# A sparse graph attention layer on one core: tiles of more than 16 slots in two chunks, the weighted sum in slot 0's buffer, the scatter behind the next gathers

## Chip, cores and metric

The kernel runs on one core of a Trainium2 chip. The metric is the device time from the first to the last instruction, in microseconds (us), as the median of several runs; less is better. The engines are TensorE (PE in the profile), VectorE (DVE), ScalarE (ACT), GpSimd (POOL) and SyncE (SP). POOL here does little arithmetic in the part that matters: it issues the indirect transfers (gathers and scatters of rows), one after the other and in a fixed order.

## What is computed

The reference is one layer of graph attention over 3327 nodes with 1024 features each:

```python
h = jnp.maximum(_layernorm(x, axis=-1), 0.0)
f = h @ Wf + bf
g = h @ Wg + bg
e = jax.nn.relu(f @ g.T)
scores = jnp.where(adj > 0, e, NEG)            # NEG = -9e15
attention = jax.nn.softmax(scores, axis=1)
x = x + attention @ (h @ W + bW)
```

The adjacency matrix is sparse: a node has some 16 neighbours, at most a few dozen. So the kernel doesn't compute 3327 x 3327 scores. It makes a list of neighbours for every node and gathers their rows.

## The kernel before

The first part, up to about 300 us, reads `x` and `adj`, writes the normalised rows to memory (`hd`), finds each node's neighbours, and sorts the nodes by their number of neighbours. It also multiplies the two score weights into one matrix, so that a score is a dot product of a projected row q with the plain row of a neighbour. There is a dense version of the whole layer too, which runs only where a node has more neighbours than the lists hold; it doesn't run on these inputs.

The second part works on 26 tiles of 128 nodes each, from many neighbours to few. `CAPS` has the number of slots of each tile: how many neighbours the node with the most of them has.

```python
CAPS = [37, 25, 23, 22, 21, 21, 20, 20, 19, 19, 18, 18, 17, 17, 17, 16, 16, 15, 15, 15, 14, 14, 13, 13, 12, 11]
ONE_CHUNK = 20
AHEAD = 3
```

For each slot k of a tile, one indirect transfer gathers 128 rows (512 KB) into a buffer G, and VectorE makes the 128 dot products with q:

```python
gpool = ctx.enter_context(tc.tile_pool(name="G", bufs=23))
ypool = ctx.enter_context(tc.tile_pool(name="y", bufs=2))
xpool = ctx.enter_context(tc.tile_pool(name="xp", bufs=2))

def prepare(s):                       # cut: the PSUM groups and the mask
    gather(pi, pd[:, :], perm[:, s : s + 1])        # neighbour lists
    gather(hp, hd[:, :], perm[:, s : s + 1])        # own rows
    ...                                             # TensorE: transpose hp, q = hp @ A   (line 667)

def dot(s, k):
    e = st[s]
    g = G[s, k] = gpool.tile([P, D], FP, name="G")
    gather(g, hd[:, :], e["pi"][:, k : k + 1])
    junk = jpool.tile([P, D], BF, name="junk")
    nc.vector.tensor_tensor_reduce(                 # line 684
        junk, g, e["q"][:, :D], 1.0, e["q"][:, D : D + 1], op0=ALU.mult, op1=ALU.add,
        accum_out=e["sc"][:, k : k + 1],
    )
```

After the last dot of a chunk the scores go through a softmax. A tile in two chunks keeps the maximum and the sum of the first, and rescales the weighted sum y when the second has a greater maximum:

```python
def softmax(s, k0, k1, last):         # cut: to what a second chunk adds
    ...
    if k0:
        nc.vector.tensor_tensor(nm, nm, e["nm"], op=ALU.min)
    nc.scalar.activation(sc, sc, AF.Exp, bias=nm, accum_out=l)
    if k0:
        nc.scalar.activation(al, e["nm"], AF.Exp, bias=nm, scale=-1.0)
        nc.vector.scalar_tensor_tensor(l, e["l"], al, l, op0=ALU.mult, op1=ALU.add)
    ...
    if k0:
        nc.scalar.activation(e["y"], e["y"], AF.Copy, scale=al)      # line 711
```

Then the rows are added up with their weights. Slot 0 is scaled into y by ScalarE, most others are added by VectorE, and some slots of the tile's last chunk are scaled by ScalarE and added by TensorE, which transposes at the same time:

```python
def on_tensor(s, k0, k1):
    m = min(max(0, CAPS[s] - 13), k1 - k0 - 2)
    ks = range(max(k0, 1), k1)
    return [k for i, k in enumerate(ks) if (i + 1) * m // len(ks) > i * m // len(ks)]

def combine(s, k0, k1, last):
    e = st[s]
    if not k0:
        e["y"] = ypool.tile([P, D], FP, name="y")
    y = e["y"]
    e["first"] = True
    pe = on_tensor(s, k0, k1) if last else []
    for k in range(k0, k1):
        p = e["sc"][:, k : k + 1]
        g = G[s, k]
        if k in pe:
            nc.scalar.activation(g, g, AF.Copy, scale=p)             # line 741
            sum_transposed(e, g, e["first"], False)                  # TensorE, line 725
            e["first"] = False
        elif k == 0:
            nc.scalar.activation(y, g, AF.Copy, scale=p)             # line 745
        else:
            nc.vector.scalar_tensor_tensor(y, g, p, y, op0=ALU.mult, op1=ALU.add)   # line 747
```

TensorE transposes y on top of its own sum and multiplies with W; the result gets the rows of x by an accumulating gather and is scattered to the output:

```python
def project(s):                       # cut
    sum_transposed(e, e["y"], e["first"], True)
    ...                                                              # yT @ W, line 759
    r = e["r"] = xpool.tile([P, O], FP, name="res")
    ...
            nc.scalar.copy(r[:, o * CB : (o + 1) * CB], ps)          # line 761

def finish(s):
    e = st[s]
    gather(e["r"], x[:, :], perm[:, s : s + 1], compute_op=ALU.add)
    ins = nc.gpsimd.indirect_dma_start(out=out[:, :], ..., in_=e["r"], ...)   # line 767
```

The order in which the work is written down:

```python
for s, cap in enumerate(CAPS):
    half = (cap + 1) // 2
    units += [(s, 0, half), (s, half, cap)] if cap > ONE_CHUNK else [(s, 0, cap)]

prepare(0)
prepare(1)
for i, (s, k0, k1) in enumerate(units):
    last = k1 == CAPS[s]
    dots(s, range(k0, k1))
    if not k0 and s:
        finish(s - 1)
    softmax(s, k0, k1, last)
    if i + 1 < len(units):
        s2, a, b = units[i + 1]
        dots(s2, range(a, min(b, a + AHEAD)))
    combine(s, k0, k1, last)
    if last:
        project(s)
        if s + 2 < NT:
            prepare(s + 2)
```

The framework puts each engine's instructions in a final order at build time: among those that its own model of time holds ready, the one written first goes first. It also hands out the buffers of a pool from those that are free at that point, not in turn. On the chip each engine then works strictly in that order.

Of the kernel before, what the change touches and what calls it, by code (L numbers as in the profile page):

```python
# [8 lines left out]
FP = mybir.dt.float32  # L9
I32 = mybir.dt.int32  # L10
AF = mybir.ActivationFunctionType
ALU = mybir.AluOpType
# [10 lines left out]
NBIN = 64  # L23

CAPS = [37, 25, 23, 22, 21, 21, 20, 20, 19, 19, 18, 18, 17, 17, 17, 16, 16, 15, 15, 15, 14, 14, 13, 13, 12, 11]
ONE_CHUNK = 20
AHEAD = 3
LAG = 4

# [260 lines left out]
def edge_path(ctx: ExitStack, tc: tile.TileContext, x, adj, Wf, bf, Wg, bg, W, bW, out, flag):  # L290
# [10 lines left out]
    nc = tc.nc  # L301
    N, D = x.shape
    O = W.shape[1]
    P = 128
# [21 lines left out]
    hd = dram.tile([N, D], FP, name="hd")  # L326
# [15 lines left out]
    perm = const.tile([P, NT], I32, name="perm")  # L342
    final = const.tile([P, 1], I32, name="final")
# [7 lines left out]
    with ExitStack() as part1:  # L351
# [73 lines left out]
        def degrees(t):  # L425
            n = rows(t)
            r = kpool.tile([P, N], FP, name="r")
            a = r.bitcast(I32)
            for b, m in pieces(t):
                nc.sync.dma_start(a[b : b + m], adj[t * P + b : t * P + b + m, :])  # L430

            cuts = [0, SEG // 2 * SW, N] if t >= NT - 2 else [0, N]
            for i, (b, e) in enumerate(zip(cuts, cuts[1:])):
                to = deg[:n, t : t + 1] if not i else half[:n]
                nc.scalar.activation(r[:n, b:e], a[:n, b:e], AF.Relu, accum_out=to)  # L435
                nc.gpsimd.tensor_mul(r[:n, b:e], r[:n, b:e], iotaj[:n, b:e])  # L436
                if i:
                    nc.scalar.activation(deg[:n, t : t + 1], deg[:n, t : t + 1], AF.Identity, bias=half[:n])
            return r
# [115 lines left out]
        for t in range(NT):  # L555
            r = degrees(t)
# [63 lines left out]
    W_sb = ctx.enter_context(tc.tile_pool(name="W", bufs=1)).tile([P, KD, O], FP, name="W_sb")  # L620
    nc.sync.dma_start(W_sb, W.rearrange("(k p) o -> p k o", p=P))
    psp = ctx.enter_context(tc.tile_pool(name="ps", bufs=3))
    gpool = ctx.enter_context(tc.tile_pool(name="G", bufs=23))
    hpool = ctx.enter_context(tc.tile_pool(name="hp", bufs=2))
    qpool = ctx.enter_context(tc.tile_pool(name="q", bufs=2))
    hTpool = ctx.enter_context(tc.tile_pool(name="hT", bufs=1))
    ypool = ctx.enter_context(tc.tile_pool(name="y", bufs=2))
    yTpool = ctx.enter_context(tc.tile_pool(name="yT", bufs=1))
    xpool = ctx.enter_context(tc.tile_pool(name="xp", bufs=2))
    jpool = ctx.enter_context(tc.tile_pool(name="junk", bufs=1))  # L630
# [4 lines left out]
    p_o = ctx.enter_context(tc.tile_pool(name="p_o", bufs=2, space=PSUM))  # L635

    def gather(to, table, idx, **kw):
        nc.gpsimd.indirect_dma_start(  # L638
            out=to,
            out_offset=None,  # L640
            in_=table,
            in_offset=bass.IndirectOffsetOnAxis(ap=idx, axis=0),
            **kw,
        )
# [8 lines left out]
    st = {}  # L653
# [23 lines left out]
    G = {}  # L677

    def dot(s, k):
        e = st[s]  # L680
        g = G[s, k] = gpool.tile([P, D], FP, name="G")
        gather(g, hd[:, :], e["pi"][:, k : k + 1])
        junk = jpool.tile([P, D], BF, name="junk")
        nc.vector.tensor_tensor_reduce(  # L684
            junk, g, e["q"][:, :D], 1.0, e["q"][:, D : D + 1], op0=ALU.mult, op1=ALU.add,
            accum_out=e["sc"][:, k : k + 1],
        )

    def softmax(s, k0, k1, last):

        e = st[s]
        sc = e["sc"][:, k0:k1]
        nc.vector.scalar_tensor_tensor(sc, sc, 0.0, e["mask"][:, k0:k1], op0=ALU.max, op1=ALU.add)
        nm = small.tile([P, 1], FP, name="nm")
        nc.vector.tensor_reduce(nm, sc, AX.X, ALU.max, negate=True)
        if k0:
            nc.vector.tensor_tensor(nm, nm, e["nm"], op=ALU.min)
        l = small.tile([P, 1], FP, name="l")
        nc.scalar.activation(sc, sc, AF.Exp, bias=nm, accum_out=l)
        if k0:  # L700
            al = small.tile([P, 1], FP, name="al")
# [3 lines that stand above are left out]
            rs = small.tile([P, 1], FP, name="rs")  # L705
            nc.vector.reciprocal(rs, l)
            if k0:
                nc.vector.tensor_tensor(al, al, rs, op=ALU.mult)
            nc.vector.tensor_scalar(sc, sc, rs, None, op0=ALU.mult)
        if k0:  # L710
            nc.scalar.activation(e["y"], e["y"], AF.Copy, scale=al)
        e["nm"], e["l"] = nm, l
# [7 lines that stand above are left out]
    def sum_transposed(e, g, first, last):  # L720

        if first:
            e["yT"] = p_y.tile([P, KD, P], FP, name="yT_ps")
        for c in range(KD):
            nc.tensor.matmul(  # L725
                e["yT"][:, c, :], g[:, c * P : (c + 1) * P], ident, is_transpose=True,
                start=(first and c % 4 == 0), stop=(last and c % 4 == 3), skip_group_check=True,
            )

    def combine(s, k0, k1, last):  # L730
        e = st[s]
        if not k0:
            e["y"] = ypool.tile([P, D], FP, name="y")
        y = e["y"]
        e["first"] = True
        pe = on_tensor(s, k0, k1) if last else []
# [4 lines that stand above are left out]
                nc.scalar.activation(g, g, AF.Copy, scale=p)  # L741
                sum_transposed(e, g, e["first"], False)
                e["first"] = False
            elif k == 0:
                nc.scalar.activation(y, g, AF.Copy, scale=p)  # L745
            else:
                nc.vector.scalar_tensor_tensor(y, g, p, y, op0=ALU.mult, op1=ALU.add)  # L747

    def project(s):
        e = st[s]  # L750
        yT = yTpool.tile([P, KD, P], FP, name="yT")
        sum_transposed(e, e["y"], e["first"], True)
        for g in range(0, KD, 4):
            nc.scalar.copy(yT[:, g : g + 4, :], e["yT"][:, g : g + 4, :])  # L754
        r = e["r"] = xpool.tile([P, O], FP, name="res")
        for o in range(OH):
            ps = p_o.tile([P, CB], FP, name="ps_o")
            for k in range(KD):
                nc.tensor.matmul(ps, yT[:, k, :], W_sb[:, k, o * CB : (o + 1) * CB], start=(k == 0), stop=False)  # L759
            nc.tensor.matmul(ps, ones3, bW3[:, o * CB : (o + 1) * CB], start=False, stop=True)  # L760
            nc.scalar.copy(r[:, o * CB : (o + 1) * CB], ps)  # L761

    def finish(s):
        e = st[s]

        gather(e["r"], x[:, :], perm[:, s : s + 1], compute_op=ALU.add)
        ins = nc.gpsimd.indirect_dma_start(  # L767
            out=out[:, :],
            out_offset=bass.IndirectOffsetOnAxis(ap=perm[:, s : s + 1] if s < N // P else final, axis=0),
            in_=e["r"],  # L770
            in_offset=None,
            bounds_check=None if s < N // P else N - 1,
            oob_is_err=s < N // P,
        )
        tc.declare_no_dep(ins.ins, group="results", reason="other rows")
        tc.add_to_no_dep_group("results", ins.ins)

# [12 lines left out]
# [3 lines that stand above are left out]
    done = set()  # L793

    def dots(s, ks):
        for k in ks:
            if (s, k) not in done:
                done.add((s, k))
                dot(s, k)
# [3 lines left out]
    for i, (s, k0, k1) in enumerate(units):  # L803
        last = k1 == CAPS[s]
        dots(s, range(k0, k1))
        if not k0 and s:
            finish(s - 1)
        softmax(s, k0, k1, last)
        if i + 1 < len(units):
            s2, a, b = units[i + 1]  # L810
            dots(s2, range(a, min(b, a + AHEAD)))
        combine(s, k0, k1, last)
        if last:
            project(s)
            if s + 2 < NT:
                prepare(s + 2)
            if s + 2 == NT - 1:
                bad = failed()
    finish(NT - 1)
    return bad  # L820


def kernel(tc: tile.TileContext, x, adj, Wf, bf, Wg, bg, W, bW, out):

    nc = tc.nc
    with tc.tile_pool(name="flag", bufs=1) as fpool:
        flag = fpool.tile([1, 1], I32, name="flag")
        bad = edge_path(tc, x, adj, Wf, bf, Wg, bg, W, bW, out, flag)  # L830
        with tc.If(bad > 0):
            dense_path(tc, x, adj, Wf, bf, Wg, bg, W, bW, out)
# [27 lines left out]
```

## Time and profile before

| | |
|---|---|
| time, median of 3 runs | 1418.14 us (1415.55 to 1426.23) |
| span of the profiled run | 1415.5 us |
| VectorE busy | 1221.1 us (86%) |
| TensorE busy | 1172.8 us (83%) |
| POOL busy | 876.6 us (62%) |
| ScalarE busy | 474.8 us (34%) |
| moved by the DMA engines | 372.52 MB, mean 263 GB/s |

A row of the profile's costliest groups gives the source line, the engine and operation, what it writes and reads, the shape and the count; then the busy time of the group, the mean time of one in ns, and how long the engine had stood idle just before them and what ended most of that. A list of waits gives who waited, for whom, the total in us, how often, and the longest. A shape such as `128x1024` is partitions by elements. The time between two scatters to the output (line 767) is a good measure of one tile. Some of them, each with the start of its scatter:

| tile | slots | chunks | scatter at us | since the one before, us |
|---|---|---|---|---|
| 2 | 23 | 2 | 531.98 | 44.4 |
| 3 | 22 | 2 | 575.52 | 43.5 |
| 4 | 21 | 2 | 616.37 | 40.9 |
| 5 | 21 | 2 | 661.43 | 45.1 |
| 6, 7 | 20 | 1 | 707.48, 754.75 | 46.1, 47.3 |
| 8, 9 | 19 | 1 | 803.58, 853.47 | 48.8, 49.9 |
| 10, 11 | 18 | 1 | 898.42, 943.45 | 45.0, 45.0 |
| 12, 13, 14 | 17 | 1 | 982.32, 1022.18, 1059.45 | 38.9, 39.9, 37.3 |
| 15, 16 | 16 | 1 | 1094.20, 1128.78 | 34.8, 34.6 |

### The profile page before, as it was taken

How to read it: one execution, taken by the hardware profiler on the slowest of the kernel's cores; microseconds unless marked ns; L12 is line 12 of the kernel's file. 1: busy time of each engine (PE TensorE's matmuls, PEld its weight loads, DVE VectorE, ACT ScalarE, POOL GpSimd, SP SyncE). 2: the span in 40 equal slices, each digit the busy share in tenths (PEclk: the TensorE clock that was granted, in tenths of full speed). 3: DMA queues.
4: the chain of work that ended last, by engine and by line, in shares of the span. 5: the costliest groups of instructions: out<-in, count | busy, mean ns of one | idle time of the engine just before them, and what ended most of it. 6: DMA issues, size and time to landing. Idle time of an engine off the chain costs nothing.

```text
span 1415.5 us, 14137 instructions
## 1 busy us (share of the span) xinstructions
PE 1172.8 (83%) x4355; PEld 684.0 (48%) x4355; DVE 1221.1 (86%) x2550; ACT 474.8 (34%) x738; POOL 876.6 (62%) x628
## 2 busy tenths in 40 slices
PE   4569998167288999999878977899999999999784
PEld 3544554044165556665545544555555555555331
DVE  4888889919979999998898788889999999999970
ACT  6666776311063244433312321222222222222110
POOL 8677777364666766775556556666667766666501
PEclk9999999578599999999989988999999999999897
DMA  9898796196678999886778667878889888888712
GB/s 370 330 356 307 294 346 229 49 361 236 227 269 289 316 315 330 282 291 224 266 284 277 192 248 265 275 233 266 256 285 304 273 265 255 256 285 286 242 31 61
DMA packets 97710, 372.52 MB, mean 263 GB/s; under 512 B 14268, under 2 KB 14684, under 8 KB 94297
## 3 DMA queue, kind: packets, MB, share of 16 engines
q0 software_dynamic: 79552, 286.85, 60.6%
q1 hardware_dynamic: 10860, 70.49, 13.2%
q10 hardware_dynamic: 7212, 14.18, 2.8%
q8 instruction: 36, 0.59, 0.2%
q14 instruction: 50, 0.41, 0.1%
HBM read 343.67 MB, written 27.80 MB: 262 GB/s over the span
## 4 chain that ended last, share of the span: by engine, by line
issue 26%; DVE 23%; PE 20%; POOL 18%; DMA 9%; ACT 4%; POOLq 0%; ACTq 0%; SPq 0%; DVEq 0%
DVE y L747 11%; POOL r L436 10%; PE ps_o L759 10%; POOL G L638 6%; DVE junk L684 6%; DMA G<-hd,pi 5%; PE ps_q L667 4%; PE yT_ps L725 3%; DMA pi<-pd,perm 2%; ACT G L741 2%; DVE cand L446 2%; PE ps_A L519 1%; DVE sc L684 1%; POOL res L638 1%; ACT r L435 1%
## 5 line engine op out<-in xcount | busy, mean ns | idle before, releaser
L638 POOL DMA_INDIRECT G<-hd,pi x468 | 542.8, 1160 | 260.0 <-issue 99.2
L684 DVE CUSTOM_DVE_ANT_0 junk<-G,q 128x1024 bf16<-128x1024 f32 x468 | 601.1, 1284 | 68.2 <-DMA G<-hd,pi 48.7
L667 PE MATMUL ps_q<-A_sb,hT 128*128 128x342 f32 x1248 | 394.2, 464 | 53.6 <-ACT q L669 43.2
L747 DVE SCALAR_TENSOR_TENSOR y<-G,sc,y 128x1024 f32<-128x1024 f32 x320 | 411.7, 1286 | 8.0 <-ACT y L745 6.1
L759 PE MATMUL ps_o<-W_sb,yT 128*128 128x512 f32 x832 | 387.6, 621 | 9.5 <-ACT yT L754 9.1
L667 PEld LDWEIGHTS ps_q<-A_sb,hT 128*128 128x128 f32 x1248 | 231.4, 193 | 172.3 <-ACT q L669 44.6
L759 PEld LDWEIGHTS ps_o<-W_sb,yT 128*128 128x128 f32 x832 | 161.2, 198 | 208.9 <-issue 190.6
L436 POOL TENSOR_TENSOR r<-r,iotaj 128x3327 f32<-128x3327 f32 (+4 forms) x28 | 188.6, 6740 | 67.0 <-ACT r L435 50.4
L446 DVE MAX8 cand<-r 128x8 f32<-128x208 f32 (+2 forms) x416 | 134.9, 363 | 35.2 <-POOL r L436 35.2
L741 ACT ACTIVATE G<-G,sc 128x1024 f32<-128x1024 f32 x122 | 129.8, 1137 | 0.0
L519 PE MATMUL ps_A<-WgT,WfT 128*128 128x512 f32 x256 | 120.7, 633 | 1.1 <-ACT WfT L490 1.0
L761 ACT COPY res<-ps_o 128x512 f32<-128x512 f32 x52 | 30.4, 585 | 269.2 <-PE ps_o L760 269.2
L725 PE MATMUL yT_ps<-ident,G 128*128 128x128 f32 x976 | 116.5, 275 | 3.2 <-ACT G L741 3.2
L725 PEld LDWEIGHTS yT_ps<-ident,G 128*128 128x128 f32 x976 | 107.0, 140 | 15.8 <-ACT G L741 7.9
L669 ACT COPY q<-ps_q 128x342 f32<-128x342 f32 x78 | 33.5, 450 | 199.3 <-DVE sc L684 94.4
L638 POOL DMA_INDIRECT res<-in_x_dram,perm x26 | 47.0, 1806 | 68.5 <-ACT res L761 65.4
L754 ACT COPY yT<-yT_ps 128x512 f32<-128x512 f32 x52 | 27.8, 587 | 166.4 <-PE yT_ps L725 166.4
L519 PEld LDWEIGHTS ps_A<-WgT,WfT 128*128 128x128 f32 x256 | 51.3, 203 | 65.0 <-issue 62.7
L725 PE MATMUL yT_ps<-ident,y 128*128 128x128 f32 x208 | 35.0, 323 | 52.3 <-DVE y L747 38.8
L435 ACT ACTIVATE r<-r 128x3327 f32<-128x3327 int32 (+4 forms) x28 | 77.5, 2766 | 0.1
L767 POOL DMA_INDIRECT out_dram<-res,perm x25 | 30.2, 1207 | 70.9 <-DMA res<-in_x_dram,perm 70.9
L651 ACT COPY hT<-ps_t 128x512 f32<-128x512 f32 x52 | 29.8, 592 | 117.6 <-PE ps_q L667 72.0
(139 smaller groups left out, 786.7 us busy)
## 6 DMA issues: line engine op xcount, KB each, us to landing
r<-in_adj_dram SPq DMA_DIRECT2D x25, 1663.5 KB, 9.6
xt<-in_x_dram SPq DMA_DIRECT2D x25, 512.0 KB, 10.2
hd<-xt ACTq DMA_DIRECT2D x25, 512.0 KB, 6.6
G<-hd,pi POOLq DMA_INDIRECT x468, 6.1
wr<-in_L_gnn_Wg_dram SPq DMA_DIRECT2D x8, 512.0 KB, 13.7
wr<-in_L_gnn_Wf_dram SPq DMA_DIRECT2D x8, 512.0 KB, 8.9
W_sb<-in_L_gnn_W_dram SPq DMA_DIRECT2D x1, 4096.0 KB, 16.6
r<-in_adj_dram SPq DMA_DIRECT2D x1, 1455.6 KB, 8.8
```

The costliest lines, as they stand in the source:

```text
L435: nc.scalar.activation(r[:n, b:e], a[:n, b:e], AF.Relu, accum_out=to)
L436: nc.gpsimd.tensor_mul(r[:n, b:e], r[:n, b:e], iotaj[:n, b:e])
L446: nc.vector.max(cand[:n, s * 8 : s * 8 + 8], r[:n, s * SW : min(N, (s + 1) * SW)])
L519: nc.tensor.matmul(ps, WfT[:, k, :], WgT[:, k, o * CB : (o + 1) * CB], start=(k == 0), stop=(k == KD - 1))
L638: nc.gpsimd.indirect_dma_start(out=to, out_offset=None, in_=table, in_offset=bass.IndirectOffsetOnAxis(ap=idx, axis=0), **kw,)
L667: nc.tensor.matmul(ps[:, :QB], hT[:, k, :], A_sb[:, k, o : o + QB], start=(k == 0), stop=False)
L669: nc.scalar.copy(q[:, o : o + QB], ps[:, :QB])
L684: nc.vector.tensor_tensor_reduce(junk, g, e["q"][:, :D], 1.0, e["q"][:, D : D + 1], op0=ALU.mult, op1=ALU.add, accum_out=e["sc"][:, k : k ...
L725: nc.tensor.matmul(e["yT"][:, c, :], g[:, c * P : (c + 1) * P], ident, is_transpose=True, start=(first and c % 4 == 0), stop=(last and c % ...
L741: nc.scalar.activation(g, g, AF.Copy, scale=p)
L747: nc.vector.scalar_tensor_tensor(y, g, p, y, op0=ALU.mult, op1=ALU.add)
L759: nc.tensor.matmul(ps, yT[:, k, :], W_sb[:, k, o * CB : (o + 1) * CB], start=(k == 0), stop=False)
```

## The change

Three things change. Tiles of 17 to 20 slots, too, are worked on in two chunks, so that the buffers of a first chunk are free again before all of the tile's dots are done. The weighted sum y isn't kept in a buffer of its own: it is kept in the buffer of slot 0, whose row it starts from, and the memory of the two y buffers goes to G, which gets 25. And the tile's end is issued elsewhere: the accumulating gather of x is written right after the product with W, and the scatter is placed behind the gathers of the next tile's first slots, so that POOL need not stand while the gather lands.

```diff
-ONE_CHUNK = 20
+ONE_CHUNK = 16
...
-    gpool = ctx.enter_context(tc.tile_pool(name="G", bufs=23))
+    gpool = ctx.enter_context(tc.tile_pool(name="G", bufs=25))
...
-    ypool = ctx.enter_context(tc.tile_pool(name="y", bufs=2))
...
     def dot(s, k):
         e = st[s]
         g = G[s, k] = gpool.tile([P, D], FP, name="G")
-        gather(g, hd[:, :], e["pi"][:, k : k + 1])
+        st["gathered"] = gather(g, hd[:, :], e["pi"][:, k : k + 1])
...
     def combine(s, k0, k1, last):
         if not k0:
-            e["y"] = ypool.tile([P, D], FP, name="y")
+            e["y"] = G[s, 0]
...
             elif k == 0:
-                nc.scalar.activation(y, g, AF.Copy, scale=p)
+                nc.scalar.activation(y, y, AF.Copy, scale=p)
...
     def project(s):
...
+        gather(r, x[:, :], perm[:, s : s + 1], compute_op=ALU.add)
+
     def finish(s):
-        e = st[s]
-
-        gather(e["r"], x[:, :], perm[:, s : s + 1], compute_op=ALU.add)
-        ins = nc.gpsimd.indirect_dma_start(
...
+        with tc.issue_after(st["gathered"].ins):
+            ins = nc.gpsimd.indirect_dma_start(
...
     for i, (s, k0, k1) in enumerate(units):
         last = k1 == CAPS[s]
         dots(s, range(k0, k1))
-        if not k0 and s:
-            finish(s - 1)
         softmax(s, k0, k1, last)
         if i + 1 < len(units):
             s2, a, b = units[i + 1]
             dots(s2, range(a, min(b, a + AHEAD)))
+        if last and s:
+            finish(s - 1)
         combine(s, k0, k1, last)
```

`tc.issue_after` orders the issue alone: the scatter goes into POOL's queue behind the last gather written so far, and waits for nothing else than before.

More of the change, by code (lines that the diff above doesn't have):

```diff
@@ L637, in gather @@
     def gather(to, table, idx, **kw):
-        nc.gpsimd.indirect_dma_start(
+        return nc.gpsimd.indirect_dma_start(
             out=to,
@@ L761, in project @@
             nc.scalar.copy(r[:, o * CB : (o + 1) * CB], ps)
+        gather(r, x[:, :], perm[:, s : s + 1], compute_op=ALU.add)
     def finish(s):
-        e = st[s]
-        gather(e["r"], x[:, :], perm[:, s : s + 1], compute_op=ALU.add)
[L767 to L774, printed above, removed]
+        with tc.issue_after(st["gathered"].ins):
+            ins = nc.gpsimd.indirect_dma_start(
+                out=out[:, :],
+                out_offset=bass.IndirectOffsetOnAxis(ap=perm[:, s : s + 1] if s < N // P else final, axis=0),
+                in_=st[s]["r"],
+                in_offset=None,
+                bounds_check=None if s < N // P else N - 1,
+                oob_is_err=s < N // P,
+            )
         tc.declare_no_dep(ins.ins, group="results", reason="other rows")
```

## The prediction

> **What bounds the kernel now.** I read the page's busy times first, then its forty slices, then cut the part that the change touches into stretches and asked for the waits in each.
>
> The page says VectorE (DVE) is busiest with 1221.1 of 1415.5 us, TensorE (PE) second with 1172.8. These are averages over two parts with different work; only the second, from the first gather at 296 us, is touched. From the costliest groups:
>
> ```profile
> L684 DVE CUSTOM_DVE_ANT_0 junk<-G,q 128x1024 bf16<-128x1024 f32 x468 | 601.1, 1284 | 68.2 <-DMA G<-hd,pi 48.7
> L747 DVE SCALAR_TENSOR_TENSOR y<-G,sc,y 128x1024 f32<-128x1024 f32 x320 | 411.7, 1286 | 8.0 <-ACT y L745 6.1
> ```
>
> These are the kernel's two big VectorE operations, one dot product per gathered slot and one weighted add per slot not given to TensorE. The reader is to see that 68.2 us of VectorE idleness stands before the dots, most of it ended by a gather landing. To see where, I cut the second part at scatters of whole tiles, at 616 us (tile 4) and at 1060 us (tile 14). Between these two lie the last two-chunk tile (21 slots) and the nine tiles of 20 to 17 slots, one chunk each today. The columns are start and end, length, then busy time of PE, PEld, DVE, ACT, POOL, then granted clock, DMA share and GB/s:
>
> ```profile
> 487.00:616.00 129.00, 122.63 (x519) 74.97 (x518) 127.32 (x205) 49.91 (x74) 90.13 (x78) 0.99 0.89 307
> 616.00:1060.00 444.00, 396.41 (x1495) 231.85 (x1494) 392.19 (x579) 123.53 (x186) 267.16 (x228) 0.94 0.77 257
> 1060.00:1334.00 274.00, 262.19 (x884) 142.42 (x882) 266.85 (x393) 58.77 (x107) 186.83 (x150) 1.00 0.85 274
> ```
>
> The first row holds three two-chunk tiles (23 to 21 slots): VectorE is 98.7% busy. The last row holds the small one-chunk tiles: 97.4%. The middle row is 88.3%: 51.8 us of VectorE are lost there, at a lower granted clock and with the DMA engines emptier. So the middle is not bound by any engine but by a wait. The waits of that stretch (total us, times, longest):
>
> ```profile
> DVE junk L684 <- DMA G<-hd,pi: 39.3, 25, 3.5
> ...
> POOL G L638 <- ACT y L745: 60.1, 10, 10.6
> ...
> POOL out_dram L767 <- DMA res<-in_x_dram,perm: 31.0, 11, 4.2
> ...
> POOL res L638 <- ACT res L761: 6.7, 6, 1.9
> ```
>
> VectorE waits for gathers, and the gathers' queue (POOL) waits about 6 us per tile for ACT line 745. That line scales slot 0 into y, and it is the first reader to finish with any G buffer of the tile. It cannot run before all dots of the tile and its softmax are done. The event in the queue's timeline, for a tile of 19 slots:
>
> ```profile
> 733.50 1.01 POOL L638 DMA_INDIRECT hp<-hd,perm  x1 [0.31 <-issue]
> 744.52 1.86 POOL L638 DMA_INDIRECT G<-hd,pi  x1 [10.01 <-ACT y L745]
> ```
>
> With this tile's slots and the next tile's first ones, all 23 buffers are full. POOL stands 10 us, and after the first buffer is freed the next gather still needs its landing time (6.1 us median on the page). VectorE meanwhile runs out of gathered rows. In 487 to 616 the same wait does not appear: chunks of 11 to 13 slots give buffers back halfway through the tile.
>
> **What the Trainium skill says.** "Perfetto Trace Analysis", section Optimization Strategy: a gap that recurs on the engine that should be saturated can mean too few buffers for the next tile. The trace agrees: about 5 us of VectorE per tile over ten tiles, with POOL waiting for a buffer. "TensorE: Matmul & The Clock Gate", section What's actually happening: an idle window of about 3.4 us drops the array to half its clock. The trace fits: in the middle stretch PE waits for y up to 6.6 us and the granted clock is 0.94 (0.89 to 0.90 between 707 and 898 us); in the saturated stretches it is 0.99 to 1.00. "DMA: Bandwidth & Descriptors", section Specifications: about 358 GB/s of HBM per core. The two-chunk stretch moves 307 GB/s with DMA engines 89% busy, so there is room, but not much. The same page, section Two DMAs through the same engine are not ordered: a dependent DMA needs its issuer to wait for the first one's semaphore. That is POOL's wait for res at line 767, 75.7 us in the whole trace.
>
> **The change, part by part.**
>
> 1. *Two chunks for 17 to 20 slots.* Nine tiles: 20, 20, 19, 19, 18, 18, 17, 17, 17. Large operations do not change in number. TensorE takes min(CAPS-13, second chunk-2) slots; the second chunks are 10, 10, 9, 9, 9, 9, 8, 8, 8, so CAPS-13 (7 down to 4) still fits. VectorE keeps CAPS dots plus 12 adds.
>  Added per tile on VectorE, from today's two-chunk tiles: a second masked max (0.17 and 0.16 us), a minimum (0.15), the sum's rescale (0.22) and one product (0.16): 0.86 us, nine times 7.7 us. On ACT: two exponentials and one rescale of y (1.15 us), about 1.9 us; ACT is 28% busy there.
>  Removed: the wait for slot 0 until 17 to 20 dots are over.
>  I size this in two ways. (a) By busy share: 392.2 + 7.7 = 399.9 us of VectorE work at the 98.7% of the two-chunk stretch is 405.2 us instead of 444: 38.8 us less. (b) By the rate of large operations. Between 487 and 616 us there are 65.5 dots (two records each) and 37 adds, 102.5 in 129 us: 1.259 us each with all overhead of two chunks. Between 1060 and 1334 there are 217 in 274: 1.263. In the middle there are 192 + 120 = 312 in 444: 1.423. At 1.26 they take 393 us: 51 us less. (a) keeps the busy time that isolated operations show (1.28 us and a record of 0.08), (b) lets dots and adds pair at 2.4 us as they do when VectorE is fed.
> 2. *y in slot 0's buffer, 25 instead of 23 + 2.* The memory is the same. y holds a G buffer until TensorE has transposed it, so 24 or 23 stay for rows. The pool gives out whichever buffer is free, so one that is held does not block those behind it in turn. For tiles up to 16 slots I count 0, at most a few us either way.
> 3. *Scatter behind gathers, accumulate-gather after project.* POOL's wait for res to land (about 2.4 us per tile) goes, and gathers fill it. But POOL is 60 to 70% busy and VectorE 97 to 99% in the stretches without the buffer wait, so it is worth little: 0 to 3 us in all. The accumulate-gather now stands before the rest of the next tile's gathers in program order; its wait for ACT res was only 6.7 us in the middle stretch and may grow.
> 4. *The end.* After 1334 us the last tiles finish on PE and POOL alone. Last res at 1397.2, last scatter at 1403.6, end at 1415.5: this chain has no other work to hide behind and nothing in the change shortens it. 0, with some us of luck in how the last tiles interleave.
>
> Sum: minus 39 to minus 51 from part 1, 0 to minus 3 from the scatter, perhaps 2 to 5 given back by the changeover from two chunks to one, which moves to 17|16. (Today's changeover tile, 616 to 661 us, took 45.1 us where its equal before took 40.9.) I take 43 us off 1418.1: 1375 us.
>
> **The rivals.**
>
> *TensorE becomes the bound.* For: a saturated tile of 21 slots took 40.9 us between scatters (575.5 to 616.4), of which PE was busy 39.0 at clock 1.00. A 20-slot tile has one transposed slot less, near 1.1 us. PE then needs some 38 to 40 us, VectorE 32 operations at 1.26, 40.3 us. They are nearly tied, and in two-chunk tiles all of TensorE's slots fall in the second chunk, so PE gets its work in bursts. Against: the three tiles between 487 and 616 us ran at 1.26 per operation with the same burst. If PE binds at 42 us or the burst costs 1.5 us per tile, 14 us of the gain are lost: 1390.
>
> *The gathers stay the limit.* For: DMA is at 89% when VectorE is fed, and POOL's queue is in order, so a wait for ACT res ahead of the gathers stalls them all. Against: POOL busy 90 of 129 us in the fed stretch, and waits for ACT res of 2 to 3 us did not starve VectorE there. If it bites, 10 to 25 us are lost: 1385 to 1400.
>
> *Chunks cost more than they bring.* The tiles of 17 lose only about 3 us each today (scatter to scatter 38.9, 39.9, 37.3), so a second softmax with its chain through ACT (VectorE to ACT and back, then y's rescale) could make these three no faster. Already half counted; 1380.
>
> **Range and chances.** Sizing (a) with a small loss gives about 1385, (b) with the scatter's help about 1365; both rivals biting together give 1400. Range 1358 to 1400. The 2% line lies at 1389.8, 15 us above my number, a little over one spread of about 14: faster 0.80, same 0.17, slower 0.03. The last would need the issue order of POOL to turn bad in many tiles, for which the profile shows nothing.
>
> **What would show it.** Right: POOL's wait for ACT line 745 falls from 67 to under 15 us; VectorE's wait for gathers falls from 48.7 to under 20; the nine tiles take 37 to 42 us between scatters; granted clock 0.97 or more from 700 to 900; POOL's wait at line 767 is near 15 us (the end only). Wrong: a new large wait of POOL for ACT res, or of PE or VectorE for each other in these tiles; or tiles of 16 and fewer slots slower than their 34 to 36 us because y holds a buffer; or a longer end.

## Result, and the profile after

The changed kernel takes 1369.88 us (median of four runs, 1367.98 to 1371.97) against 1416.85 us for the kernel before beside it (1414.42 to 1426.23). The ratio is 0.9657, with a 95% interval of 0.961 to 0.9704. A later repeat on another chip gave 0.9658.

The first rows to look at are again VectorE's two large operations, from the costliest groups of the changed kernel. The two numbers after the bar are busy time and mean time of one, then comes the idle time before them:

```profile
L683 DVE CUSTOM_DVE_ANT_0 junk<-G,q 128x1024 bf16<-128x1024 f32 x468 | 599.4, 1281 | 35.3 <-ACT q L668 18.1
L746 DVE SCALAR_TENSOR_TENSOR G<-G,sc 128x1024 f32<-128x1024 f32 x320 | 410.8, 1284 | 4.6 <-ACT G L744 4.1
```

Counts and durations are what they were. What went is idle time: before the dots it is 35.3 us instead of 68.2, and gathers no longer head the list of what ended it. Over the whole span VectorE's idle time is 1370.1 - 1218.5 = 151.6 us; before it was 1415.5 - 1221.1 = 194.4. That is 42.8 of the 45.4 us by which the two profiled spans differ.

To see where, the span is cut at the scatters of the same tiles as before: 0, 4, 14 and 22.

| stretch between scatters | before, us | after, us | difference |
|---|---|---|---|
| start to tile 0 (37 slots, two chunks in both) | 439.33 | 445.96 | +6.6 |
| tiles 1 to 4 (two chunks in both) | 177.0 | 176.7 | -0.4 |
| tiles 5 to 14 (nine of the ten changed to two chunks) | 443.1 | 386.7 | -56.4 |
| tiles 15 to 22 (16 to 13 slots, one chunk in both) | 274.1 | 276.7 | +2.6 |
| tile 22 to the end | 82.0 | 84.1 | +2.1 |

The sum is -45.4 us. The whole gain lies where the change was aimed, though not all of the 56.4 is gain. At a cut VectorE is already ahead with the next tiles' dots, and with two chunks it is less far ahead. By the counts of the groups it does 189 dots and 116 adds in the third stretch, 305 in place of 312; 221 instead of 217 in the fourth, and 34 instead of 31 in the last. Seven large operations, some 9 us, are passed on. What remains is about 47 us of gain in the third stretch, and the last two are no slower than their extra operations explain. Whether the first row is the change's isn't shown: the changed kernel, profiled again, has that scatter at 446.7 us, and four programs that differ from it only in later tiles have it at 437 to 442 us.

The same cut with busy times (columns as in the prediction: start and end, length, busy time of PE, PEld, DVE, ACT, POOL, granted clock, DMA share, GB/s), for the changed kernel:

```profile
494.00:623.00 129.00, 122.69 (x518) 74.98 (x517) 127.32 (x203) 49.91 (x74) 90.63 (x80) 0.99 0.90 312
623.00:1009.00 386.00, 375.36 (x1493) 222.35 (x1492) 380.90 (x616) 138.74 (x222) 264.39 (x223) 1.00 0.87 290
1009.00:1286.00 277.00, 264.56 (x883) 143.74 (x881) 272.42 (x397) 58.30 (x105) 186.97 (x152) 0.98 0.84 275
1286.00:1370.00 84.00, 53.16 (x128) 23.80 (x128) 41.66 (x52) 9.83 (x18) 12.19 (x10) 0.81 0.26 70
```

The second row now looks like the first. VectorE is busy 380.90 of 386 us (98.7%, before 88.3%), the clock is 1.00 (before 0.94), and the DMA engines are at 0.87 (before 0.77). 386 us for 305 large operations are 1.266 us each (before 1.423), the rate that the neighbouring stretches had all along.

The waits of that stretch, 623 to 1009 us (total, times, longest):

```profile
POOL G L637 <- DVE G L746: 35.5, 36, 9.0
...
POOL out_dram L768 <- DMA res<-in_x_dram,perm: 24.5, 10, 4.1
...
DVE df L670 <- DMA pi<-pd,perm: 3.8, 1, 3.8
...
POOL res L637 <- ACT res L760: 3.1, 2, 2.2
```

POOL's wait for the scaling of slot 0 (60.1 us here before) is down to one of 0.3 us. In its place POOL waits for the first adds, and that starves nobody: VectorE's wait for gathers, 39.3 us here before, doesn't occur once. One line hardly moved: POOL still stands behind the landing of x, ten times here (24.5 us; before eleven times, 31.0) and 26 times in the whole trace (77.5 us; before 75.7).

### The profile page after: what moved, and what is told of

Same layout as the page of the kernel before. It is cut to its first block, busy times and chain, and to the rows that moved or that the text cites. A ratio compares the mean times of both kernels' runs of the same rounds, so it can differ in the third digit from the quotient of the medians.

```text
span 1370.1 us, 14184 instructions
## 1 busy us (share of the span) xinstructions
PE 1154.2 (84%) x4355; PEld 676.0 (49%) x4355; DVE 1218.5 (89%) x2595; ACT 489.2 (36%) x774; POOL 875.0 (64%) x628
## 4 chain that ended last, share of the span: by engine, by line
PE 43%; issue 14%; DVE 9%; DMA 4%; POOL 4%; ACT 2%; POOLq 0%; ACTq 0%; DVEq 0%
PE ps_q L666 18%; PE ps_o L758 17%; PE yT_ps L724 6%; DVE G L746 5%; DMA G<-hd,pi 4%; POOL G L637 3%; DVE junk L683 3%; PE ps_q L667 1%; PE ps_o L759 1%; ACT hT L650 1%; DMA pi<-pd,perm 1%; PE ps_t L649 1%; DVE sc L683 1%; POOL res L637 0%; ACT q L668 0%
## 5 line engine op out<-in xcount | busy, mean ns | idle before, releaser
L683 DVE CUSTOM_DVE_ANT_0 junk<-G,q 128x1024 bf16<-128x1024 f32 x468 | 599.4, 1281 | 35.3 <-ACT q L668 18.1
L666 PE MATMUL ps_q<-A_sb,hT 128*128 128x342 f32 x1248 | 399.2, 467 | 59.4 <-ACT q L668 41.8
L746 DVE SCALAR_TENSOR_TENSOR G<-G,sc 128x1024 f32<-128x1024 f32 x320 | 410.8, 1284 | 4.6 <-ACT G L744 4.1
L758 PE MATMUL ps_o<-W_sb,yT 128*128 128x512 f32 x832 | 374.8, 604 | 4.4 <-ACT yT L753 4.4
L758 PEld LDWEIGHTS ps_o<-W_sb,yT 128*128 128x128 f32 x832 | 156.5, 192 | 195.4 <-issue 182.3
L724 PE MATMUL yT_ps<-ident,G 128*128 128x128 f32 x1184 | 146.2, 279 | 24.7 <-DVE sc L708 8.2
L724 PEld LDWEIGHTS yT_ps<-ident,G 128*128 128x128 f32 x1184 | 133.8, 143 | 41.8 <-issue 15.7
L637 POOL DMA_INDIRECT res<-in_x_dram,perm x26 | 46.2, 1776 | 67.4 <-ACT res L760 62.8
L768 POOL DMA_INDIRECT out_dram<-res,perm x25 | 34.5, 1378 | 72.5 <-DMA res<-in_x_dram,perm 72.5
L435 ACT ACTIVATE r<-r 128x3327 f32<-128x3327 int32 (+4 forms) x28 | 77.5, 2768 | 0.1
L637 POOL DMA_INDIRECT hp<-hd,perm x26 | 26.8, 1032 | 35.0 <-DVE final L612 21.2
L649 PE MATMUL ps_t<-ident,hp 128*128 128x128 f32 x208 | 31.2, 292 | 15.7 <-issue 10.8
## 6 DMA issues: line engine op xcount, KB each, us to landing
wr<-in_L_gnn_Wg_dram SPq DMA_DIRECT2D x8, 512.0 KB, 13.9
```

The lines of the kernel that those rows point to most:

```text
L637: return nc.gpsimd.indirect_dma_start(out=to, out_offset=None, in_=table, in_offset=bass.IndirectOffsetOnAxis(ap=idx, axis=0), **kw,)
L649: nc.tensor.transpose(ps[:, k, :], of[:, (g + k) * P : (g + k + 1) * P], ident)
L666: nc.tensor.matmul(ps[:, :QB], hT[:, k, :], A_sb[:, k, o : o + QB], start=(k == 0), stop=False)
L683: nc.vector.tensor_tensor_reduce(junk, g, e["q"][:, :D], 1.0, e["q"][:, D : D + 1], op0=ALU.mult, op1=ALU.add, accum_out=e["sc"][:, k : k ...
L724: nc.tensor.matmul(e["yT"][:, c, :], g[:, c * P : (c + 1) * P], ident, is_transpose=True, start=(first and c % 4 == 0), stop=(last and c % ...
```

## Experiments

### The three parts of the change, one by one

One chip measured four versions. It was slower and less steady than the others (the kernel before took 1458.96 us there, 1455.06 to 1474.41), so effects of a per cent aren't readable from the totals; the stretches inside the profiles show more. The ratios leave out runs more than 1.5% slower than the fastest of the same version (two of four of the scatter alone, one of four of chunks and buffers), while the times are medians of all runs of a version.

**Chunks alone** (23 + 2 buffers and the scatter as before):

```diff
-ONE_CHUNK = 20
+ONE_CHUNK = 16
```

> The kernel before with one edit: tiles of more than 16 slots in two chunks; 23 row buffers, two buffers of y and the scatter stay as they were. Theory (a first chunk hands buffers back in mid-tile, and that is the whole gain): 34 to 48 us less than before, so 0.966 to 0.976 of its time, and POOL's wait for ACT line 745 gone. Rival (the two more row buffers matter as much): 15 to 25 us less. Rival (the scatter's place matters): at least 10 us slower than the full change.

**Buffers alone:**

```diff
-    gpool = ctx.enter_context(tc.tile_pool(name="G", bufs=23))
-    ypool = ctx.enter_context(tc.tile_pool(name="y", bufs=2))
+    gpool = ctx.enter_context(tc.tile_pool(name="G", bufs=25))
...
-            e["y"] = ypool.tile([P, D], FP, name="y")
+            e["y"] = G[s, 0]
```

> The kernel before with y in slot 0's buffer and 25 row buffers; tiles of 17 to 20 slots in one chunk, scatter as before. Theory (a tile in one chunk holds all its buffers until its last dot): two more gathers fit ahead (about 2.4 us of dots per tile), but the first buffer is now freed by the first add of VectorE, about 1.3 us after the scaling of slot 0; net some 1 us in each of nine tiles, 3 to 20 us less than before. Rival (too few buffers, however they are used): most of the gain, 30 us or more. Second rival (y holding a buffer costs): slower than before.

**Scatter alone** (the gather of x written in `project`, the scatter under `issue_after` and after the next tile's first dots):

```diff
     def finish(s):
-        gather(e["r"], x[:, :], perm[:, s : s + 1], compute_op=ALU.add)
+        with tc.issue_after(st["gathered"].ins):
...
-        if not k0 and s:
-            finish(s - 1)
...
+        if last and s:
+            finish(s - 1)
```

> The kernel before with only the end of a tile placed as in the changed kernel: accumulating gather of x right after the product with W, scatter issued behind the next tile's first gathers. Theory: the scatter lands where it was, two gathers behind the gather of x, because those gathers are issued long before; 0 plus or minus 4 us, and POOL still waits about 75 us in total for the gather of x. Rival (it takes the wait away): 10 us or more less, and that wait near 15 us.

**Chunks and buffers**, that is, the change without its third part:

> Two chunks and y in slot 0's buffer with 25 row buffers, the end of a tile as in the kernel before. Theory: within 4 us of the full change (1370 us). Rival (the scatter's place brings part of the gain): 8 us or more slower than the full change.

| version | time, us | ratio to before, with interval | tiles 5 to 14 in its profile, us |
|---|---|---|---|
| before | 1458.96 | | |
| chunks alone | 1430.2 | 0.9782 (0.9718 to 0.9846) | 408.6 |
| buffers alone | 1446.23 | 0.9909 (0.984 to 0.9977) | 449.2 |
| scatter alone | 1460.88 | 0.9908 (0.98 to 1.0016) | 451.3 |
| chunks and buffers | 1424.47 | 0.9716 (0.9635 to 0.9796) | 395.7 |

The windows of that stretch in the four, in the table's order (columns as above):

```profile
642.00:1051.00 409.00, 384.01 (x1491) 224.97 (x1490) 380.81 (x616) 138.87 (x222) 272.82 (x224) 0.97 0.83 273
```

```profile
638.00:1087.00 449.00, 392.99 (x1484) 229.13 (x1484) 390.03 (x578) 122.02 (x186) 270.74 (x229) 0.93 0.77 254
```

```profile
625.00:1076.00 451.00, 394.53 (x1487) 231.47 (x1488) 389.33 (x573) 122.91 (x186) 264.69 (x227) 0.92 0.75 253
```

```profile
650.00:1045.00 395.00, 377.30 (x1488) 222.51 (x1488) 380.52 (x615) 138.90 (x222) 267.09 (x223) 0.99 0.85 282
```

The two versions without chunks stay near the length, the VectorE share (86 to 87%; before 88%) and the low clock of the kernel before. The two with chunks leave it. So the chunks carry the gain, and two more buffers for rows don't replace them. Waits in the stretch of the second version:

```profile
POOL G L637 <- DVE G L746: 69.2, 28, 11.3
...
DVE junk L683 <- DMA G<-hd,pi: 33.3, 22, 5.5
```

Counting the gathers in POOL's queue shows that all buffers were in use. At each of POOL's waits of more than 4 us for a buffer in this stretch, the kernel before had asked for exactly 23 rows of the tile at work and the next one, and the version with more buffers for exactly 25. But with y in slot 0's buffer, the first buffer to come back is that of the first add (line 746), no longer that of slot 0, so this version has more buffers and a later return at once. A pool much larger than 25 wasn't tried.

Chunks alone have no wait of VectorE for gathers in the stretch. Two details differ from what was expected. POOL's wait for slot 0 is not gone: 19.9 us of it stay there, and VectorE doesn't run out of rows. And by the medians the gain is 28.8 us, less than the 34 to 48 expected, though the stretch itself is 42.7 us shorter than that of the scatter alone; the first part is longer, with its first scatter at 461 us where the scatter alone has it at 436.

The scatter needs no statistics. The version with the scatter alone has, engine by engine, the same instructions in the same order with the same operands and waits as the kernel before; the version without the scatter has those of the changed kernel (so its 1424.47 us says how this chip differs from the one that gave 1369.88, not what the scatter is worth). **The third part of the change does nothing to the program.** The gather that the scatter of tile s is told to follow is the third one of tile s + 2, and in POOL's queue of the kernel before that gather already stood ahead of it, by one gather for tile 0 and by 3 to 17 for the later ones. In both kernels, nearly always until the last three tiles, the queue reads: gather of x, two other gathers, scatter. In the changed kernel, at a tile's end (start, duration, idle before):

```profile
733.34 1.74 POOL L637 DMA_INDIRECT G<-hd,pi  x1 [0.67 <-DVE G L746]
735.38 1.57 POOL L637 DMA_INDIRECT res<-in_x_dram,perm  x1 [0.30 <-issue]
737.26 1.47 POOL L637 DMA_INDIRECT G<-hd,pi  x1 [0.30 <-issue]
739.03 0.96 POOL L637 DMA_INDIRECT G<-hd,pi  x1 [0.30 <-issue]
742.59 1.09 POOL L768 DMA_INDIRECT out_dram<-res,perm  x1 [2.60 <-DMA res<-in_x_dram,perm]
```

From the gather of x to the scatter are 7.2 us. Issuing this gather and two others fills 4.6 of them; POOL stands for the other 2.60. The scatter-alone version is therefore a second measurement of the kernel before. Its ratio of 0.9908, with an interval that holds 1, shows what a ratio on that chip is worth (by all runs its median is 0.1% higher): the 0.9909 of the buffers can't be told from nothing.

Does the buffer part add to the chunks? The intervals of the versions with and without it overlap. In the profiles the stretch is 408.6 - 395.7 = 12.9 us shorter with it, and without it there is a wait that the other hardly has. Chunks alone, waits of VectorE between 642 and 1051 us:

```profile
DVE y L747 <- ACT y L745: 13.7, 3, 6.1
```

The first add of a tile stands up to 6.1 us behind ScalarE's scaling of slot 0. In that longest case ScalarE was itself idle for 9.1 us ahead of its copy of the tile before's transposed sum, and the scaling came right after it. With y in slot 0's buffer the same wait (on line 744) is 0.9 us, and all idle time before the adds is 8.8 us instead of 18.0. Why isn't shown: there, too, ScalarE stands up to 8.6 us ahead of such a copy. The small tiles differ as well: tiles 15 to 22 take 297.1 us with chunks alone and 279.7 with both, for 224 large operations each. But this is one profile each, and that of both parts is of its fastest run (1409.25 us; the next took 1423.58). So these differences are an indication and not a measurement.

### The scatter moved in earnest

If the constraint bound nothing, what is the wait worth? Here each of the scatters of tiles 0 to 22 is written among the gathers of a later tile, at a table's place six or seven gathers (five for tile 22) behind its gather of x; the last three stay.

```diff
     def dot(s, k):
...
         st["gathered"] = gather(g, hd[:, :], e["pi"][:, k : k + 1])
+        if (s, k) in OUT_AT:
+            finish(OUT_AT[s, k])
...
-        if last and s:
+        if last and s > 23:
             finish(s - 1)
```

> The changed kernel with each scatter placed six gathers behind its gather of x instead of two, so that what it waits for has landed when POOL comes to it. Theory (POOL has slack): POOL's wait at the scatter falls from 77 us to about 20 us (the last three tiles only), and the time stays within 6 us of the changed kernel, 0.961 to 0.970 of the kernel before. Rival (POOL's standing there delays gathers that VectorE needs): 10 to 30 us less than the changed kernel, under 0.958.

It ran on a second chip, as did the two runs with slots moved to and from TensorE and the one with two chunks for every tile (the kernel before: 1418.55 us, 1415.34 to 1421.08). 1361.53 us, ratio 0.9598 (0.9574 to 0.9621), which lies between the two expectations. It was repeated on a third chip beside the changed kernel itself:

> The changed kernel as it is, beside the next three on one chip: 0.961 to 0.970 of the kernel before, as at first. It is the measure for the three others of this set.

> The changed kernel with each scatter six gathers behind its gather of x, once more and now beside the changed kernel. If the 8 us that it was faster are real (POOL standing 2.4 us per tile holds back some gathers): 5 to 11 us less than the changed kernel. If they were the chip's: within 3 us of it.

The kernel before took 1418.01 us there (1411.5 to 1424.47), the changed kernel 1373.18 us, ratio 0.9658 (0.9609 to 0.9706), and the moved scatter 1363.06 us, 0.9598 (0.9557 to 0.964). Both times the ratio is 0.006 lower than the changed kernel's, some 8 us (10.1 by the two medians on the third chip), though the intervals of the ratios overlap. From tile 0's gather of x to the end, which leaves out the varying start, its two profiles are 6.2 and 3.3 us shorter than the changed kernel's; the second is of its slowest run. In its first profile POOL's wait for x is the end's three alone, and what POOL waits for instead is the adds:

```profile
POOL G L638 <- DVE G L749: 119.8, 99, 7.6
...
POOL out_dram L771 <- DMA res<-in_x_dram,perm: 14.6, 3, 5.1
```

63 us of waiting went from one line; 26 of them came back on the adds and 16 on ScalarE's copies of the result (79.3 us instead of 62.8). What VectorE got of it is seen in two fixed windows, 445 to 1000 and 1000 to 1300 us. First the changed kernel, then the moved scatter:

```profile
445.00:1000.00 555.00, 534.69 (x2156) 318.73 (x2157) 548.08 (x885) 205.16 (x321) 384.65 (x330) 0.99 0.88 299
1000.00:1300.00 300.00, 281.63 (x944) 154.13 (x943) 295.40 (x427) 63.22 (x114) 195.35 (x160) 0.97 0.83 269
```

```profile
445.00:1000.00 555.00, 539.94 (x2196) 321.99 (x2195) 552.57 (x890) 206.45 (x322) 376.81 (x332) 1.00 0.87 300
1000.00:1300.00 300.00, 281.98 (x926) 151.88 (x924) 296.45 (x427) 61.51 (x112) 204.28 (x153) 0.97 0.79 261
```

VectorE works 552.57 + 296.45 = 849.0 instead of 843.5 us of the 855; in the repeated pair 847.5 instead of 841.9. That is 5.5 and 5.6 us less idle. The rest wasn't traced to a place. The order of other instructions shifts with the scatter, too, so this is the worth of the whole new order.

### Is TensorE the bound now?

The prediction's first rival. Two runs move slots of the nine tiles between the engines; each slot is one add of VectorE or eight transposing matmuls of TensorE and one scaling of ScalarE.

```diff
-        m = min(max(0, CAPS[s] - 13), k1 - k0 - 2)
+        m = min(max(0, CAPS[s] - (15 if 17 <= CAPS[s] <= 20 else 13)), k1 - k0 - 2)
```

> The changed kernel with two slots fewer per tile on TensorE in the nine tiles of 20 to 17 slots (CAPS-15 instead of CAPS-13), so two more adds on VectorE in each. If VectorE sets the pace there (98.7% busy): two times 1.2 us times nine, about 20 us more (15 to 24) than the changed kernel. If TensorE sets it: up to 19 us less, as each slot takes some 1.1 us off it. If both: 12 to 22 us more.

The other run has 12 in place of 15, one slot more for TensorE:

> The changed kernel with one slot more per tile on TensorE in the nine tiles of 20 to 17 slots, so one add fewer on VectorE in each. If VectorE alone sets the pace: 8 to 11 us less than the changed kernel. If TensorE (97.2% busy there) sets it: 5 to 10 us more. If the two are tied: within 4 us.

Two slots less on TensorE: 1394.49 us, ratio 0.9809 (0.9768 to 0.985), and tiles 5 to 14 take 412.2 us, 25.5 more than in the changed kernel. VectorE does 325 large operations there instead of 305, at 1.268 us each: the rate is unchanged, so VectorE sets the pace. By the ratios the total is 22 us more than the changed kernel's, as expected for that case. One slot more: the stretch takes 377.2 us, 9.5 less, with 294 operations at 1.282. At the old rate eleven fewer would have saved 13.9 us; PE begins to hold VectorE up. And the second run's total is 1376.46 us, ratio 0.9703 (0.9682 to 0.9725), no gain: by the ratios some 7 us more than the changed kernel, with intervals that overlap. That is the size expected with TensorE as the pace, but it doesn't arise in these tiles. Its windows, cut at the scatters of tiles 4, 14 and 22:

```profile
614.00:991.00 377.00, 369.95 (x1510) 220.43 (x1509) 369.27 (x600) 146.21 (x226) 255.75 (x223) 1.00 0.87 298
991.00:1284.00 293.00, 280.37 (x941) 152.64 (x939) 279.45 (x407) 60.99 (x110) 182.30 (x153) 0.99 0.79 261
```

In the first row PE (98.1%) and DVE (97.9%) are level: with this slot the balance is used up. The second row is 16 us longer than its equal in the changed kernel (277). Of these, 279.45 - 272.42 = 7.0 us are more VectorE work (225 large operations instead of 221, passed on from the stretch before), and 9.0 us are new idle time. Waits of VectorE from 980 to 1220 us in this run:

```profile
DVE df L670 <- DMA pi<-pd,perm: 8.1, 3, 3.8
```

In the changed kernel that line has 1.6 us. The neighbour list is fetched late, behind gathers in POOL's queue. Since the order of the following tiles' instructions changed as well, it isn't settled that this is all of the loss.

### The other tiles, and the end

**Two chunks for every tile**, which asks whether 16 is the right border:

```diff
-ONE_CHUNK = 16
+ONE_CHUNK = 10
```

> The changed kernel with every tile in two chunks, also the eleven of 16 to 11 slots. Theory (these tiles don't wait for buffers, VectorE is 97% busy in them): the second softmax costs 0.86 us of VectorE each, 9.5 us in all, so 5 to 15 us more than the changed kernel. Rival (chunks help wherever they are): 5 us or more less.

1367.12 us, ratio 0.9655 (0.9611 to 0.97): no difference from the changed kernel (0.9657), so neither expectation held. Tiles 15 to 22 take 6.9 us less (269.8), but VectorE also does 6 large operations fewer in them (215 instead of 221), which are 7.5 us; tiles 23 to 25 take 6.6 us more (78.8 instead of 72.2). The work was passed on and none saved. The second chunks cost nothing either: VectorE's busy time is 1218.5 us, as in the changed kernel, in spite of 55 more instructions.

**The end.** In the last 84 us TensorE is busy 53 and VectorE 42 (fourth row of the windows above). Five slots of each of the last four tiles go to TensorE:

```diff
-        m = min(max(0, CAPS[s] - 13), k1 - k0 - 2)
+        m = min(max(0 if s < 22 else 5, CAPS[s] - 13), k1 - k0 - 2)
```

> The changed kernel with five slots on TensorE in each of the last four tiles (13, 13, 12, 11 slots), which have none there now. Theory (at the end TensorE waits for y: 8.2, 7.2 and 4.2 us in the profile of the changed kernel, with nothing beside it): 5 to 12 us less than the changed kernel. Rival (the product with W, some 15 us per tile, fills TensorE there and the extra transposes come on top): within 3 us or slower.

1370.77 us, ratio 0.9665 (0.9619 to 0.9711): nothing. Its window from the scatter of tile 22:

```profile
1277.00:1366.00 89.00, 68.26 (x248) 36.84 (x246) 37.39 (x54) 20.75 (x30) 12.82 (x10) 0.91 0.23 64
```

Tile 22 ends 9 us earlier, but 7.3 of these come from the start (first scatter at 438.7 us instead of 446.0). Between the scatters of tiles 14 and 22 VectorE does 206 instead of 221 large operations and still takes 275.4 us instead of 276.7; one wait of 9.1 us for ScalarE's copy of a q uses up half of what was saved. Then PE has 15 us more to do where it alone decides, and the end takes 88.7 us instead of 84.1.

**All that helped**: the moved scatter, two chunks down to 14 slots, and the last tiles' slots.

```diff
-ONE_CHUNK = 16
+ONE_CHUNK = 13
...
+        if (s, k) in OUT_AT:
+            finish(OUT_AT[s, k])
...
+        m = min(max(0 if s < 22 else 5, CAPS[s] - 13), k1 - k0 - 2)
```

> All that pointed to a gain together: late scatters, five slots on TensorE in the last four tiles, and two chunks for tiles of 14 to 16 slots too. If the parts add up (8 us, 5 to 12 us and about 3 us): 1348 to 1357 us, 0.950 to 0.957 of the kernel before. If they take the same idle time from each other: 1358 to 1365 us.

1354.71 us (1352.64 to 1358.83), ratio 0.9535 (0.9493 to 0.9577): the best of all versions, with its median in the expected range. Tiles 5 to 14 take 380.7 us and tiles 15 to 22 257.3 instead of 276.7, with 199 large operations in them instead of 221, so at 1.293 us each instead of 1.252. In the last stretch VectorE has 28 instead of 34, and PE is the busier engine:

```profile
1270.00:1357.00 87.00, 66.36 (x242) 35.91 (x240) 36.74 (x54) 20.25 (x29) 10.28 (x8) 0.91 0.25 70
```

It is 18 us under the changed kernel on the same chip, of which the moved scatter alone brings 10 there. The last tiles' slots brought nothing measurable alone, and neither did two chunks for every tile; two chunks down to 14 slots alone, and two of the three parts together, weren't tried.

## Why the prediction was right, and where not

The time, 1369.88 us, lies 5 us from the 1375 and well inside 1358 to 1400.

**What bounds the kernel: held.** POOL's 10 us stand behind slot 0's scaling, with all buffers full, was the cause. Chunks alone remove VectorE's wait for gathers in the stretch, more buffers alone don't. The Trainium skill says in "Perfetto Trace Analysis", section Optimization Strategy, that a gap that recurs on the engine that should be saturated can mean too little memory for the next tile. That fits, with one addition that the runs show: two more buffers, the first of them returned by an add, did not help measurably where returning the old ones earlier did. The clock followed: 0.94 to 1.00 in the stretch. This is in line with the skill's "TensorE: Matmul & The Clock Gate", section What's actually happening, by which an idle window of about 3.4 us lowers it: PE's waits for y, up to 6.6 us in the stretch before, are gone, and its longest wait there is now 3.3 us.

**Step 1, two chunks: held.** Between the scatters the gain is 56.4 us, and about 47 when the seven operations passed on are taken out; 39 to 51 was said. Of the two ways to size it the rate was the better one: 1.266 us for each large operation against 1.26 assumed. The busy share of 98.7% came out exactly, but it was applied to a busy time that doesn't stay (see the last section).

**The changeover's 2 to 5 us: not a loss.** The first one-chunk tile, tile 15, took 44.6 us between scatters instead of 34.8, but VectorE was busy 42.94 us of them: it did the dots of the next tiles that it used to have done already. Tiles 15 to 22 together take 277 us for 221 operations, 1.253 each, before 274 for 217, 1.263. The prediction had put today's slow changeover tile down as a cost of changing over; a tile's time between scatters mixes cost with work done ahead.

**Step 2, buffers: open in size.** "0, at most a few us either way" was said of the tiles up to 16 slots. By the medians chunks with buffers are 5.7 us faster than chunks alone, with overlapping intervals. The single profiles point to more, 12.9 us in tiles 5 to 14 and 17 in tiles 15 to 22, but the one with buffers is of that version's fastest run. The adds' wait for ScalarE's scaling of slot 0, the largest visible part, wasn't counted in the prediction.

**Step 3 failed.** It said that POOL's wait for res to land "goes, and gathers fill it", leaving 15 us. It stayed: 77.5 us against 75.7. The step took the diff's intent for its effect. `issue_after` names a gather that already stood earlier in the queue, and the profile before could have shown it: each scatter up to tile 23 was already behind that gather. The step's worth was mis-sized as well: moved in earnest, it points to 8 to 10 us (with intervals that overlap) and not 0 to 3. VectorE at 97 to 99% left room for more than the argument allowed. The total came out right without this step because it was put at 0 to 3 us.

**Step 4, the end: held.** From the last scatter to the end 11.9 us both times, from tile 22 to the end 84.1 us instead of 82.0.

**The rivals.** TensorE did not become the bound, but it came next: 97.2% busy in the stretch, and one slot more makes it level with VectorE. The chain that ended last now runs over PE for 43% of the span, before for 20%. Read alone, that would name PE as the bound; the run that gives PE less to do and takes 25.5 us more in the stretch shows that it isn't. The gathers as the limit fell: no wait for them is left there. That chunks cost more than they bring fell: the tiles of 17 slots take 37.0, 35.1 and 36.7 us, before 38.9, 39.9 and 37.3.

**The signs.** POOL's wait for the scaling of slot 0 and VectorE's for gathers (15.6 us in the whole trace, before 48.7) fell as said; the clock rose as said. The nine tiles take 35.1 to 43.2 us between scatters where 37 to 42 was said. POOL's wait at the scatter is the sign that failed.

## What to carry to other kernels

Where a pool of buffers runs full, ask which event returns the first one, and how much work must be over before it; bringing that event forward (here, half a tile earlier) was worth more than two more buffers. Before crediting a reordering, look at the queue that it yields: a constraint behind something already issued changes nothing. And in a queue that issues in the order written, put a dependent transfer as many transfers behind its predecessor as the landing takes: here six or seven gathers took the wait away, and two did not.

## What the runs showed of the hardware that was not expected

- The same kernel took 1416.85 us, 1418.55 us and 1418.01 us in three sets but 1458.96 us on one chip, 3% more, and there the same program in two versions came out at a ratio of 0.9908 (0.98 to 1.0016).
- VectorE's two large operations keep their own duration (1281 and 1284 ns; before 1284 and 1286), and yet the busy time of the whole span fell by 2.6 us while 45 small operations were added, which one by one had been worth 7.7. Added up one by one, all VectorE records are 1401.6 us before and 1401.9 after, as others got a little shorter (the two large groups by 2.6 us), and 183.4 us of them overlap instead of 180.5. So a busy time can't be carried over from a starved stretch to a fed one, but a rate per large operation could (1.259 and 1.263 us in the fed stretches before, 1.266 here).
- Programs that differ only in later tiles can begin differently: the first tile's scatter came between 437 and 450 us in the profiles of three sets, and on the slower chip at 436 us for the kernel before's own program but at 456 to 464 us for the three that differ from it. The cause wasn't found.
